# A table of rank shifts in a planned kernel, replaced by another table

## The chip, the cores and the metric

The kernel runs on one core of one Trainium2 chip. The metric is the device time of one execution in microseconds. Before the change the median of 14 runs is 2530.8 us, the lowest 2529.6 and the highest 2535.07.

## The reference, cut to what matters

A block of four residual steps on x of shape (4, 512, 512), each on a layer norm of x: a sparse attention whose mask comes from a small network over all pairs of rows, a feed-forward net, a differential attention, and the same feed-forward net again.

```python
# step 1, sparse attention (D = 512, 32 heads of 2, the 51 best of 512 keys per row)
h    = xn @ W1.T                                                  # 512 x 128 a batch
pair = relu(h[:, :, None, :] - h[:, None, :, :] + b1)             # 512 x 512 x 128
pair = relu(einsum('bijf,gf->bijg', pair, W2) + b2)               # 512 x 512 x 64
sim  = einsum('bijg,og->bijo', pair, W3)[..., 0] + b3[0]
_, top_idx = top_k(sim.at[:, diag, diag].set(0.0), 51)
out  = softmax(q k / sqrt(2) + mask) v @ Wout + bout
# step 2 and step 4, feed-forward (512 -> 2 x 2048 -> 512)
out  = (silu(x Wgate) * (x Wup)) @ Wdown
# step 3, differential attention (16 heads)
out  = softmax(q1 k1 * s - lam * (q2 k2 * s)) v * (1 - li) @ W_proj
```

## The kernel before

**What is tiled how.** For each batch b (0 to 3) and each of its four row tiles, `pair_group` (L751) works on two rows at a time. Two VectorE instructions make the tile `m` (128x512 each), six half-width matmuls (128 rows by 64 columns, fp16 in high and low parts) make `z`, and ScalarE makes `r` from `z`. In five of the sixteen row tiles every fourth group has its `m` made by ScalarE and its `z` by fp32 matmuls. `pair_sums` (L787) then reduces four `r` with four quarter-width matmuls (32 columns, fp32) into `sim`. `topk_tile` (L809) finds the 51 best of a finished `sim` on VectorE in seven rounds, gathers their keys and values with indirect DMAs issued by GpSimd, and does the softmax on VectorE. The feed-forward nets (`ffn`, L931) and the second attention (`attn_b`, L1017) use full-width matmuls, apart from the products with v, which are quarter-width.

A feed-forward net goes over 16 chunks of 128 hidden units. A chunk loads its weights (tile `w`), makes gate and up (`z`), and multiplies the upper half of the rows on with the down weights (accumulators `a`). The other half of its hidden values is stored to DRAM (`hk`) and comes back later (`hc`), with the down weights a second time (`we`), for a second pass (accumulators `b`).

**Names.** Net and attention tiles carry a letter and the batch: f1z is gate and up of the first net of batch 1, e3b the second pass of the second net of batch 3, b2st the scores of the attention of batch 2. `z`, `m`, `r`, `sim` without a letter are the pair work.

**What sets the order.** No engine's order follows the order of the program text. Every operation is first recorded as a task (class `Plan`, L107), with its engine, a cost from a formula (`cost`, L148), the tasks it depends on, and its tiles. `Plan.run` (L261) then plays the whole list as a list scheduler: a free engine takes the ready task of the smallest rank. On TensorE it also models the width of the array in use. To go to another width it waits until all running matmuls have ended and `DRAIN` = 0.1 us more (L327), and tasks of the present width are favoured by `STICK` = 8 (L318). A half-clock state of TensorE, a DMA queue and buffer reuse are modelled too. `Plan.issue` (L363) runs this five times forwards, each time with ranks from a backward run; at the end the ranks of the best plan get a constant added by part of the program, and the list is played once more:

```python
if r > rounds:
    rank = [t + SHIFT.get(part(task[3][0].tensor.name), 0.0) for t, task in zip(best[2], tasks)]
key = {m: min(rank[i] for i in t["tasks"]) for m, t in self.tiles.items()}
tags = {k: (b, sorted(ms, key=key.get) if r else ms) for k, (b, ms) in self.tags.items()}
order, start, length = self.run(rank, after, npre, tags, stick=self.STICK)
if best is None or length < best[0]:
    best = (length, order, rank)
```

So the shifted plan is taken only where the planner holds it shorter. The instructions are then issued in the order of the best plan from one place (L411), so all rows of the profile carry that line; each engine executes its own instructions strictly in that order. A rank is a time in us of the plan, and a shift of +40 lets a part yield to everything whose rank is less than 40 us later.

`part` (L73) maps a tile's name to a key of `SHIFT` (L53). Keys: `f`/`e` with batch and `n` (layer norm), `u`, `v` (chunks 0 to 7 and 8 to 15 of the first pass), `a` (its accumulators), `b` (the second pass); `b` with batch and `n`, `q`, `s`, `t`, `p` (norm, projections, scores, products, output); `p` with batch, row tile and half for the pair groups; `s` for their sums; `k` for the top-k of a row tile; `q`, `a`, `y`, `X` for parts of the preparation and output of step 1; `w` and `c` for scales and constants.

Of the kernel before, what the change touches and what calls it, by code (L numbers as in the profile page):

```python
# [44 lines left out]
def _size(dt):  # L45
# [5 lines left out]


SHIFT = {  # L53
    "X0": -16, "X1": -43, "X2": -35, "X3": -35, "a0": -71, "a1": -41, "a2": -39, "a3": -48, "b0n": 10,
    "b0p": -2, "b0q": 16, "b0s": -14, "b0t": -19, "b1n": -40, "b1p": -36, "b1q": -1, "b1s": -34, "b1t": -37,
    "b2n": 13, "b2q": 16, "b2s": -19, "b2t": -20, "b3n": -17, "b3p": 17, "b3q": -9, "b3s": -25, "b3t": -16,
    "c": -67, "e0a": 36, "e0b": 37, "e0n": 18, "e0u": 22, "e0v": 18, "e1a": -13, "e1b": 31, "e1n": -39,
    "e1u": -27, "e1v": -30, "e2a": 25, "e2b": 439, "e2n": -8, "e2u": -11, "e2v": 15, "e3a": 351, "e3b": 380,
    "e3n": 27, "e3u": 63, "e3v": 260, "f0a": 7, "f0b": 4, "f0n": 21, "f0u": 32, "f1a": -14, "f1n": -36,
    "f1u": -19, "f1v": -33, "f2a": 26, "f2b": 13, "f2n": 27, "f2u": 22, "f2v": 20, "f3a": -18, "f3b": -21,  # L60
    "f3n": -39, "f3u": -48, "f3v": -29, "k00": 13, "k01": 24, "k02": 26, "k03": 12, "k10": 50, "k11": 104,
    "k12": 66, "k13": 25, "k20": 28, "k21": 20, "k22": 19, "k23": 76, "k30": 54, "k31": 59, "k32": 70,
    "k33": 84, "p00u": -9, "p00v": -10, "p01u": 17, "p01v": 16, "p02u": 9, "p02v": 7, "p03u": 6, "p03v": 6,
    "p10u": 6, "p10v": 10, "p11u": 3, "p11v": 6, "p12u": -2, "p12v": -1, "p13u": 10, "p13v": 10, "p20u": 8,
    "p20v": 6, "p21u": -1, "p21v": -3, "p22v": -9, "p23u": -18, "p23v": 17, "p30u": 6, "p30v": 3, "p31u": -11,
    "p31v": -9, "p32u": -6, "p32v": 5, "p33u": 8, "p33v": 49, "q0": -17, "q1": 49, "q2": -87, "q3": -94,
    "s00": -358, "s01": -310, "s02": -192, "s03": -207, "s10": -196, "s11": -177, "s12": -37, "s13": 6,
    "s20": 2, "s21": -7, "s22": -2, "s23": 15, "s30": 1, "s31": -13, "s32": -14, "s33": 5, "w": 84, "y0": -82,
    "y1": 272, "y2": -299, "y3": -48,
}  # L70


# [1229 lines left out]
```

## Time and profile before

| what | value |
|---|---|
| median of 14 runs | 2530.8 us |
| the profiled execution's own time | 2535.03 us |
| its span, first to last instruction | 2533.3 us |
| TensorE busy | 2501.5 us, 15044 matmul records |
| VectorE busy | 2009.6 us |
| ScalarE busy | 1515.8 us |
| GpSimd busy | 966.6 us |
| bytes moved by DMA | 317.79 MB, mean 125 GB/s |

The profiled execution took 4.2 us more than the median, 1.7 us of it outside the span. A matmul that takes 379 ns from start to end does not hold the array that long: in a dense stretch the next starts some 216 ns later, and half-width matmuls run two and quarter-width ones four beside each other. A busy TensorE therefore says only that matmuls were under way.

### The profile page before, as it was taken

How to read it: one execution, taken by the hardware profiler on the slowest of the kernel's cores; microseconds unless marked ns; L12 is line 12 of the kernel's file. 1: busy time of each engine (PE TensorE's matmuls, PEld its weight loads, DVE VectorE, ACT ScalarE, POOL GpSimd, SP SyncE). 2: the span in 40 equal slices, each digit the busy share in tenths (PEclk: the TensorE clock that was granted, in tenths of full speed). 3: DMA queues.
4: the chain of work that ended last, by engine and by line, in shares of the span. 5: the costliest groups of instructions: out<-in, count | busy, mean ns of one | idle time of the engine just before them, and what ended most of it. 6: DMA issues, size and time to landing. Idle time of an engine off the chain costs nothing.

```text
span 2533.3 us, 42662 instructions
## 1 busy us (share of the span) xinstructions
PE 2501.5 (99%) x15044; PEld 1024.6 (40%) x15044; DVE 2009.6 (79%) x5164; ACT 1515.8 (60%) x2831; POOL 966.6 (38%) x847
## 2 busy tenths in 40 slices
PE   8999999999999999999999999999999999999998
PEld 4433333444343334444444333344444443443443
DVE  8889999999899999798686899977856555573531
ACT  6999998656468976443343689643422376586220
POOL 0276767475534155656624234465550000000000
PEclk9999999999999999999999999999999999999999
DMA  5432321157642022336535421034665535423446
GB/s 182 156 106 87 100 63 35 53 163 240 219 136 61 28 65 90 117 116 203 165 94 158 120 53 43 22 115 148 205 206 180 153 120 175 151 95 123 131 144 197
DMA packets 223628, 317.79 MB, mean 125 GB/s; under 512 B 29969, under 2 KB 150865, under 8 KB 222390
## 3 DMA queue, kind: packets, MB, share of 16 engines
q1 hardware_dynamic: 197302, 261.54, 32.4%
q0 software_dynamic: 26112, 53.53, 7.3%
q8 instruction: 118, 1.93, 0.3%
q14 instruction: 96, 0.79, 0.1%
HBM read 263.43 MB, written 51.39 MB: 124 GB/s over the span
## 4 chain that ended last, share of the span: by engine, by line
PE 74%; DVE 19%; DMA 4%; issue 2%; POOL 1%; ACT 1%; SPq 0%; DVEq 0%; POOLq 0%; ACTq 0%
PE z L411 19%; DVE m L411 8%; PE sim L411 6%; PE e0z L411 3%; PE e1z L411 3%; PE e2z L411 3%; PE e3z L411 3%; PE f1z L411 3%; PE f3z L411 3%; PE f2z L411 3%; DVE g L411 3%; PE f0z L411 2%; DVE b1s L411 2%; DVE b0s L411 1%; POOL g L411 1%
## 5 line engine op out<-in xcount | busy, mean ns | idle before, releaser
L411 DVE TENSOR_SCALAR m<-hw 128x512 f32<-128x512 f32 x1888 | 809.8, 483 | 60.3 <-PE z L411 58.5
L411 PE MATMUL z<-m,w2s 128*64 128x512 f16 x5664 | 750.2, 391 | 3.1 <-DVE m L411 1.7
L411 ACT ACTIVATE r<-z,zb 128x512 f32<-128x512 f32 x944 | 613.8, 698 | 222.3 <-PE z L411 160.3
L411 POOL DMA_INDIRECT g<-kv,ix x432 | 494.1, 1144 | 363.8 <-DVE ix L411 212.3
L411 POOL DMA_INDIRECT g<-kv,idx x384 | 461.8, 1203 | 417.7 <-DVE idx L411 197.8
L411 PEld LDWEIGHTS <-w2s 128*64 128x64 f16 x5688 | 315.7, 108 | 491.5 <-issue 227.3
L411 PE MATMUL sim<-r,w 128*32 128x512 f32 x2048 | 274.3, 604 | 0.0
L411 ACT ACTIVATE m<-h 128x512 f32<-128x512 f32 x160 | 107.9, 744 | 5.4 <-PE z L411 5.4
L411 PE MATMUL f3z<-f3xt,f3w 128*128 128x512 f16 x384 | 103.0, 379 | 0.1
L411 PE MATMUL e2z<-e2xt,e2w 128*128 128x512 f16 x384 | 101.5, 379 | 0.0
L411 PE MATMUL f2z<-f2xt,f2w 128*128 128x512 f16 x384 | 98.4, 379 | 0.8 <-DMA f2w<-wf 0.8
L411 DVE TENSOR_TENSOR g<-g,sc 128x832 f32<-128x832 f32 (+3 forms) x128 | 98.5, 783 | 0.3
L411 PE MATMUL z<-m,h 128*64 128x512 f32 x320 | 98.7, 594 | 0.0
L411 PE MATMUL f1z<-f1xt,f1w 128*128 128x512 f16 x384 | 98.3, 379 | 0.0
L411 PE MATMUL f0z<-f0xt,f0w 128*128 128x512 f16 x384 | 90.8, 379 | 0.2 <-ACT f0w L411 0.2
L411 PE MATMUL e0z<-e0xt,e0w 128*128 128x512 f16 x384 | 90.9, 379 | 0.0
L411 PE MATMUL e1z<-e1xt,e1w 128*128 128x512 f16 x384 | 89.5, 379 | 0.0
L411 PEld LDWEIGHTS sim<-r,w 128*32 128x32 f32 x2048 | 41.5, 108 | 115.4 <-issue 96.2
L411 PE MATMUL e3z<-e3xt,e3w 128*128 128x512 f16 x384 | 85.7, 379 | 0.0
L411 DVE MAX8 vm<-sims 128x8 f32<-128x512 f32 x112 | 76.6, 685 | 3.5 <-POOL sims L411 3.0
L411 DVE FIND_INDEX8 ix<-vm,sims 128x8 uint32<-128x512 f32 x112 | 76.4, 682 | 0.0
L411 DVE TENSOR_TENSOR g<-g,q 128x832 f32<-128x832 f32 x64 | 63.9, 999 | 6.7 <-DMA g<-kv,ix 5.6
(643 smaller groups left out, 3779.8 us busy)
## 6 DMA issues: line engine op xcount, KB each, us to landing
f0wr<-wf SPq DMA_DIRECT2D x48, 256.0 KB
wn<-wgu SPq DMA_DIRECT2D x32, 256.0 KB
wf<-f0w SPq DMA_DIRECT2D x16, 512.0 KB
e0w<-wf SPq DMA_DIRECT2D x16, 512.0 KB
f1w<-wf SPq DMA_DIRECT2D x16, 512.0 KB
e1w<-wf SPq DMA_DIRECT2D x16, 512.0 KB
f2w<-wf SPq DMA_DIRECT2D x16, 512.0 KB
f3w<-wf SPq DMA_DIRECT2D x16, 512.0 KB
```

The source lines that it names most:

```text
L411: getattr(eng, op)(*a, **k)
```

## The change

The dictionary `SHIFT` is replaced, and nothing else. The table before has 138 keys, the new one 142; a key that is missing counts as 0. No operation, tile, buffer or dependency is added or removed, and the planner's code and constants stay as they are. What changes are the ranks of the last planning round, and through them the order of instructions on each engine, and which tile takes which buffer when.

New less old value, key by key, has the median +29.5. A constant added to all ranks changes no order, so what counts is the distance from that. Most keys lie within some 20 us of it (the pair groups of batches 1 to 3 at +10 to +41 but for one at -37, the first net of batch 2 at +44 to +52). The ones far from it are these:

| part | old | new |
|---|---|---|
| sums of batch 0, s00 to s03 | -358, -310, -192, -207 | -1313, -1031, -945, -602 |
| top-k k00, k01, k02 | 13, 24, 26 | -325, -46, -58 |
| top-k k21, k22 | 20, 19 | 197, 139 |
| second net of batch 1: e1n, e1u, e1v, e1a, e1b | -39, -27, -30, -13, 31 | 100, 104, 91, 134, 98 |
| second net of batch 2, second pass: e2b | 439 | 230 |
| second net of batch 3: e3n, e3u, e3v, e3a, e3b | 27, 63, 260, 351, 380 | 232, 304, 303, 462, 483 |
| attention output of batch 3: b3p | 17 | 240 |
| keys and values q0, q1, q3 | -17, 49, -94 | -123, 161, 167 |

The diff, cut to some of its lines:

```diff
 SHIFT = {
-    "X0": -16, "X1": -43, "X2": -35, "X3": -35, "a0": -71, "a1": -41, "a2": -39, "a3": -48, "b0n": 10,
...
-    "e1u": -27, "e1v": -30, "e2a": 25, "e2b": 439, "e2n": -8, "e2u": -11, "e2v": 15, "e3a": 351, "e3b": 380,
-    "e3n": 27, "e3u": 63, "e3v": 260, "f0a": 7, "f0b": 4, "f0n": 21, "f0u": 32, "f1a": -14, "f1n": -36,
...
-    "s00": -358, "s01": -310, "s02": -192, "s03": -207, "s10": -196, "s11": -177, "s12": -37, "s13": 6,
...
+    "c": -26, "e0a": 46, "e0b": 46, "e0n": 6, "e0u": 7, "e0v": 54, "e1a": 134, "e1b": 98, "e1n": 100,
+    "e1u": 104, "e1v": 91, "e2a": -1, "e2b": 230, "e2n": 22, "e2u": 31, "e2v": 27, "e3a": 462, "e3b": 483,
+    "e3n": 232, "e3u": 304, "e3v": 303, "f0a": 40, "f0b": 30, "f0n": 34, "f0u": 52, "f0v": 45, "f1a": -9,
...
+    "q1": 161, "q2": -86, "q3": 167, "s00": -1313, "s01": -1031, "s02": -945, "s03": -602, "s10": -129,
...
 }
```

## The prediction

> **What bounds the kernel now.** I read four views. First the page's busy times and its 40 slices: they say which engine has no room.
>
> ```profile
> span 2533.3 us, 42662 instructions
> PE 2501.5 (99%) x15044; PEld 1024.6 (40%) x15044; DVE 2009.6 (79%) x5164; ACT 1515.8 (60%) x2831; POOL 966.6 (38%) x847
> PE   8999999999999999999999999999999999999998
> DVE  8889999999899999798686899977856555573531
> PEclk9999999999999999999999999999999999999999
> ```
>
> TensorE is under way 99% of the span at full clock, VectorE is full in the first half and has room in the second. So the end is set by what TensorE has to do, by how tightly it does it, and in places by VectorE. The second view is TensorE's own waits: who made it idle.
>
> ```profile
> engine line waited for: us in total, times, longest us
> PE f0b L411 <- DMA f0hc<-f0hk: 2.5, 1, 2.5
> PE z L411 <- DVE m L411: 1.7, 5, 0.7
> PE e3b L411 <- DMA e3hc<-e3hk: 1.5, 1, 1.5
> PE e1b L411 <- DMA e1we<-wf: 1.2, 1, 1.2
> PE b1s L411 <- DMA b1qks<-b1qkd: 1.2, 1, 1.2
> ```
>
> The list is short: span less busy time is 31.8 us. From the timeline of TensorE, 8.3 us of that come before 33 us (loading and preparing batch 0), 4.3 after the last matmul. About 19 us of idle time lie in the 2500 us between.
>
> The third view is the timeline of TensorE in a stretch in which only pair work runs.
>
> ```profile
> 1617.43 1.07 PE L411 MATMUL sim<-r,w 128*32 128x512 f32 x8
> 1618.42 3.13 PE L411 MATMUL z<-m,w2s 128*64 128x512 f16 x25
> 1621.48 1.06 PE L411 MATMUL sim<-r,w 128*32 128x512 f32 x8
> 1622.48 2.91 PE L411 MATMUL z<-m,w2s 128*64 128x512 f16 x23
> 1625.32 1.06 PE L411 MATMUL sim<-r,w 128*32 128x512 f32 x8
> ```
>
> This is where the time is that an order can change. Eight fp32 records of quarter width go four beside each other: 2 slots of 512 columns at 1200 a microsecond are 0.85 us, but the next width starts 1618.42 - 1617.43 = 0.99 us later. A stretch of 23 half-width records is 23 x 0.2133 / 2 = 2.45 us and takes 2.84. Each change of the array's width costs something.
>
> I summed this over all 15044 records of the trace. At those rates (512 columns in 0.2133 us for fp16, 0.4267 for fp32, by their share of the array's width) they need 2293 us. The span is 240 us longer. The width changes 936 times; from the last slot's end to the first start of the next width it is 106 ns in the mean, 99 us in all. The rest of the 240 is some 26 us of idle time inside the sequence, 4 after the last matmul, and 111 us inside the stretches: a few ns for each record, and columns that stand empty at a stretch's end.
>
> The fourth view is busy time by stage. Its columns are the window, its length, busy time of TensorE, weight loads, VectorE, ScalarE and GpSimd with instruction counts, clock, DMA share, GB/s.
>
> ```profile
> 33.00:480.00 447.00, 444.99 (x3212) 173.58 (x3211) 428.53 (x1075) 404.41 (x721) 260.11 (x216) 1.00 0.29 93
> 720.00:960.00 240.00, 236.89 (x1628) 87.34 (x1628) 238.77 (x624) 194.78 (x379) 101.61 (x86) 1.00 0.25 75
> 669.00:676.00 7.00, 4.54 (x26) 1.56 (x25) 6.65 (x25) 1.27 (x2) 4.01 (x5) 0.98 1.00 325
> 676.00:679.50 3.50, 3.50 (x10) 1.29 (x11) 2.08 (x8) 1.52 (x2) 2.03 (x3) 0.56 1.06 367
> ```
>
> In the first stage (pair work of batch 0) and under the attentions, VectorE has no idle time worth the name. The last two rows are the one event of their kind: TensorE waits 2.5 us for f0hc with the DMA engines full, and the next 3.5 us run at a granted clock of 0.56.
>
> **The change part by part.** Nothing is added or removed, so the 2293 us of matmul time stay, and so do the 2010 us of VectorE. No instruction and no DMA is new; they are moved past one another. The common drift of about +30 us costs and gives nothing. The rest acts on four terms.
>
> Term 1, width changes. How much can an order alone move? The kernel holds stages of like work, in like company, in different orders. I counted in each the width changes and the time above the 2293 us kind of sum. Second net of batch 0, first and second of batch 1, all under pair work: 34, 30 and 24 changes per 100 us (82, 69 and 49 of them in 242, 229 and 202 us). Attention of batches 0 and 1: 66 and 80 (148 and 159 in 225 and 198 us). If each went at the better twin's density, that is 82 - 58 = 24, 69 - 55 = 14 and 159 - 131 = 28, together 66 fewer; at the worse one, 20, 9 and 31, together 60 more. A change costs 0.106 us of gap at least. From above, the loss per change of whole stages: 15.0 us / 71 changes = 0.21 from 1170 to 1400. Between nets late in the span, 1.8% loss at no change (f2) and 4.0% at 15 per 100 us (f3) make 0.15, which I take. That is -10 us to +9 us. The planner that reads the new table charges 0.1 us for each change, and its operation costs agree with the trace: VectorE's `m` costs 70 + 512/1920 + 60 = 397 ns by its formula and follows its predecessor every 396 ns in the trace; a gather has 1.25 us there and follows its predecessor after 1.255 where nothing holds it up. A table that the planner holds shorter should therefore have fewer changes on the chip too, and an in-order queue doesn't lose that again. I take two thirds of the better end: -7 us.
>
> Term 2, TensorE's 19 us of waits. Bounds: all gone, -19; or as much again, +19. I take 0, because the planner sees such waits in both orders and has left few.
>
> Term 3, the tail. e2b gets 209 less and e3's chunks 43 to 241 more, so e2b goes ahead of e3z instead of standing between e3a and e3b (2476 to 2522 us now). Its 96 matmuls at 0.216 us are 20.7 us that move, not time that is saved. What may vanish are the waits there, 0.9 for e2hc and 1.5 for e3hc: -2.4. What may come is in the slower rival below. I take half of the gain, -1 us.
>
> Term 4, VectorE-bound stages. From 33 to 480 us VectorE is busy 428.5 of 447 us. The top-k of row tile 0 (k00, -338) moves forward within this stage, whose VectorE work is the same; aop, which needs all four top-ks, starts at 441 us now. At best the stage loses its 18.5 us of gaps, at worst as much comes in. That is two-sided, and I take 0. e1 is set back by some 100 us against the pair work beside it (its first pass by 121 to 147, less the 25 of that work). If pair work then ran alone that long, the loss of its stage, 61.7 of 447 us = 13.8%, would stand in place of the 6.3% that I count under e1: +7.5 us. The part of e1 that then runs without pair work goes at f2's 1.8%: -4.5. Together +3 at most; a part with a later rank still fills idle slots, so 0.
>
> The sums of batch 0 (s00 to s03) were 192 to 358 us ahead of everything already; going further ahead alters next to nothing, 0.
>
> Sum: -7 + 0 - 1 + 0 + 0 = -8 us. The profiled execution's 2535.0 would be 2527; on the median, 2530.8 - 8 = 2522.8, and I say 2522.5.
>
> A rule that speaks against this: the Trainium skill, page "TensorE: Matmul & The Clock Gate", Part 1, says that the clock falls to one half after at least one idle window of some 3.4 us, and rises after one busy window. The trace differs: 2.5 us of waiting were enough for 3.4 us at half clock. By the page, new waits under 3.4 us would cost their own length only (2.5 us for one like f0hc); by the row they cost more, which the next part prices.
>
> **The rivals.** (a) Slower: the tail's round trip is exposed. In the chain of waits, e3's second pass waits at the end for its stored halves: a DMA piece of 3.70 and one of 5.35 us. Today e2b's matmuls stand in between and leave 1.5 us visible. With e2b gone, the cover is e3's own earlier chunks. It decides when fewer than 9.05 / 0.216 = 42 matmuls are ready between the last e3z chunk and the load it needs, for instance because the hidden values have five buffers, and loads for later chunks stand behind a store that isn't ready on SP's queue. Then 9.05 us come in, and after such a wait the half clock: the 12 f0b records after the f0hc wait took 4.2 us where 12 x 0.216 = 2.6 are due, so +1.6. Together +10.7. A tail like that is likeliest where term 1 brings nothing either, so I price it alone: 2530.8 + 10.7 = 2541.5. For it: e3b waits here now. Against: 15 earlier chunks have 90 matmuls, 19 us.
>
> (b) The order is no better on the chip: what the plan gained in one place it lost in waits that the plan doesn't price. Three to four small DMA waits of the common size here (0.6 to 1.2 us, as b1s and b0s) weigh up the 8 us with one more of the f0hc kind (2.5 + 1.6). 2531, within 0.2%. For it: the DMA engines are full at some points, where a time by formula must be off. Against: only 19 us of waits in an order from the same planner.
>
> (c) The table doesn't do what it says: if the planner held the shifted list longer than its last unshifted one, the kernel would be issued without shifts. Then term 1 at its worse end: +9, 2540. The code would have to meet a table that fits it badly, so this is small.
>
> (d) Slower by scattered width changes: a plan with fewer waits bought by more changes, again term 1 at its worse end with some waits of term 2: +5 to +15, 2540.
>
> **How the numbers follow.** Forecast, faster by -5 to -20 (the better end of term 1 with part of term 2): 0.47. (b): 0.14. (a): 0.17. (d): 0.18. (c): 0.04. What a measurement of this kernel can tell from no change is about 0.2%, 5 us. Faster 0.47, same 0.14, slower 0.39. The time is that of the likeliest, 2522.5; its own range is 2511 to 2525.7. For 8 in 10: a tenth is left below, -23 us (term 1's 10 and two thirds of term 2's 19), 2508; and a tenth above, (d)'s upper end, 2545.
>
> **What the profile would show.** Term 1: fewer than 936 width changes, near 890, most of it missing under the attentions of batches 0 and 1 and under e0 and f1; the sum of 2293 us unchanged. Term 2: span less busy TensorE time still near 32 us. Term 3: e2b ends before e3z is half done, and e3b alone stands at the end without a wait over 1.5 us. Term 4: VectorE's work from 33 us to the first aop the same, that stage ending within 10 us of now. A wait of e3b for e3hc of 5 us or more speaks for (a); new rows of 2 us with stretches of half clock for (b); more than 960 changes for (c) or (d). The forecast is wrong if the changes don't fall, or if they fall and the idle time grows by as much.

## The result, and the profile after

The changed kernel is slower: 2555.6 us median (2552.77 to 2557.21) against 2531.4 for the kernel before, measured in alternation with it. The ratio is 1.0092 (95% interval 1.0082 to 1.0102). The forecast was 2522.5, faster, with a range of 2508 to 2545; sign and range are both wrong.

What the two pages share, seen after:

```profile
span 2556.4 us, 42718 instructions
...
PE 2504.0 (98%) x15044; PEld 1028.0 (40%) x15044; DVE 2019.1 (79%) x5164; ACT 1517.4 (59%) x2831; POOL 970.3 (38%) x847
...
PE   8999999999999999999999999999999999999999
...
DVE  8799999999999999886778999996666556475332
...
PEclk9999999999999999999999999999999999999999
```

The slices show nothing: 23.1 us in 2556 are spread too thin for tenths. The sum does. Span less busy time of TensorE was 31.8 us and is 52.4, which makes 20.6 us of new idle time. TensorE's time at half clock rose from 6.25 to 18.2 us. The last of it (2.84 us before, 1.11 after) lies behind the last matmul and costs nothing. In the rest TensorE did 1.7 us of matmul work before and 6.2 after, which took twice as long there, so 4.5 us more are lost. There are 856 width changes instead of 936. Without the waits that end at a few of them, which are idle time and counted already, their gaps fell from 93.6 to 85.0 us: -8.5. The 2293 us of matmul time are the same. That makes 16.6 of the 23.1 us; the other 6.5 lie inside the stretches of one width and are not split up here. TensorE's own waits name the new idle time:

```profile
engine line waited for: us in total, times, longest us
PE z L411 <- DVE m L411: 6.7, 11, 2.5
PE e1b L411 <- DMA e1we<-wf: 5.6, 7, 1.7
PE zp L411 <- DVE hw L411: 5.3, 2, 4.9
PE e1z L411 <- DMA e1w<-wf: 3.5, 2, 2.2
PE b1s L411 <- DMA b1qks<-b1qkd: 2.8, 1, 2.8
PE f0b L411 <- DMA f0we<-wf: 2.0, 2, 1.1
```

Before, `z<-m` stood at 1.7 us, e1we at 1.2, b1qks at 1.2, and zp and e1w were not among the first. No single wait explains it: VectorE is late with `m`, and loads are late in several places.

Where in time? I compared the two runs at equal matmul work done (the running sum of the 2293 us). After is 5.5 us behind when 25 us of work are done; 6.8 at 125, 15.9 at 225 and 25.8 at 325, which is 411 us into the run. It gets some back, holds 16 to 20 us until 1475 us of work, and goes to 23 at 1675 and about 25 at the end. So there are three places.

**The start.** These are TensorE's timeline rows (start, duration, engine, line, operation, count, idle before and releaser) of after, with two windows of busy time by engine:

```profile
32.34 0.42 PE L411 MATMUL zp<-hw,w2s 128*64 128x256 f16 x2 [4.93 <-DVE hw L411]
...
1768.28 2.65 PE L411 MATMUL e1z<-e1xt,e1w 128*128 128x512 f16 x7 [2.24 <-DMA e1w<-wf]
```

```profile
28.00:38.20 10.20, 5.64 (x28) 2.99 (x30) 8.31 (x24) 9.43 (x23) 0.00 (x0) 0.50 0.83 300
1700.00:1822.00 122.00, 118.52 (x587) 52.11 (x582) 86.52 (x210) 41.20 (x75) 66.94 (x66) 0.99 0.52 158
1822.00:1900.00 78.00, 72.17 (x337) 32.73 (x336) 50.68 (x103) 15.26 (x28) 44.64 (x43) 1.00 0.74 230
```

Around a wait of 4.93 us TensorE runs 10.2 us at a granted clock of 0.50 (first window): the clock falls 0.6 us after the wait has begun and rises some 6 us after it has ended. The plan holds this delay too and is still 4.6 us shorter than the old one.

**150 to 410 us.** The top-k of batch 0 gathers its rows with GpSimd's indirect DMAs, and VectorE's products wait for them. VectorE's and then GpSimd's timeline rows of one such case, after:

```profile
243.22 0.74 DVE L411 SCALAR_TENSOR_TENSOR f0w<-f0wr,sc,f0w 128x512 f16<-128x512 f32 x1
246.25 1.03 DVE L411 TENSOR_TENSOR g<-g,q 128x832 f32<-128x832 f32 x1 [2.29 <-DMA g<-kv,ix]
```

```profile
229.86 1.09 POOL L411 DMA_INDIRECT g<-kv,idx  x1 [1.42 <-DVE idx L411]
231.26 4.97 POOL L411 DMA_INDIRECT g<-kv,idx  x1 [0.30 <-issue]
```

One gather took 4.97 us instead of the 1.0 of its neighbours, the queue behind it is late, and VectorE stands 2.29 us. VectorE is the full engine of this stage and its queue is in order: `m` is late, and then `z`. The group row of these products tells the sum over the whole run (busy, mean ns, idle before and its causes), before and then after:

```profile
L411 DVE TENSOR_TENSOR g<-g,q 128x832 f32<-128x832 f32 x64 | 63.9, 999 | 6.7 <-DMA g<-kv,ix 5.6 <-issue 1.0
```

```profile
L411 DVE TENSOR_TENSOR g<-g,q 128x832 f32<-128x832 f32 x64 | 63.9, 999 | 24.6 <-DMA g<-kv,ix 11.2 <-issue 11.0 <-DMA g<-kv,idx 2.3
```

The same rows up to 410 us alone, before and then after:

```profile
L411 DVE TENSOR_TENSOR g<-g,q 128x832 f32<-128x832 f32 (+1 forms) x13 | 13.0, 997 | 0.3 <-DMA g<-kv,ix 0.3
```

```profile
L411 DVE TENSOR_TENSOR g<-g,q 128x832 f32<-128x832 f32 (+1 forms) x12 | 12.0, 1000 | 8.3 <-DMA g<-kv,ix 5.1 <-issue 3.2
```

So 8.3 of the 24.6 us belong to this stage. "issue" stands for a wait whose end the profile puts down to nothing. Here it is a wait for gathers too: 10.7 of the 11.0 us lie under a wait of VectorE's queue for the semaphores of the gathers.

Long gathers are no more frequent than before (over 2 us: 29 of 816 before, 32 after). Nor are they random: in after_half_w (experiment 4), which issues the same order, 31 of these 32 gathers are over 2 us again, 28 of the 32 within 0.3 us of their time here. What differs in the plan is the room: 19 of the 64 products stood within 0.5 us of the planned landing of their last gather before, 39 after.

**1700 to 1900 us.** In the two last windows above TensorE is busy 118.52 and 72.17 us. The same windows before:

```profile
1700.00:1822.00 122.00, 120.72 (x683) 50.07 (x680) 93.86 (x234) 50.52 (x84) 65.33 (x61) 1.00 0.52 161
1822.00:1900.00 78.00, 77.24 (x362) 35.23 (x361) 49.48 (x104) 15.06 (x32) 45.37 (x44) 1.00 0.69 216
```

The shares of the DMA engines (last column but one) are alike or a little higher after. e1 now begins at 1708 us instead of 1641 and overlaps f2, which begins at 1827 in both, until 1891 instead of 1843; the waits for e1w and e1we lie here.

### The profile page after: what moved, and what is told of

Its sections match the earlier page's. It is cut to its first block, busy times and chain, and to the rows that moved or that the text cites. A ratio compares the mean times of both kernels' runs of the same rounds, so it can differ in the third digit from the quotient of the medians.

```text
span 2556.4 us, 42718 instructions
## 1 busy us (share of the span) xinstructions
PE 2504.0 (98%) x15044; PEld 1028.0 (40%) x15044; DVE 2019.1 (79%) x5164; ACT 1517.4 (59%) x2831; POOL 970.3 (38%) x847
## 3 DMA queue, kind: packets, MB, share of 16 engines
q1 hardware_dynamic: 197302, 261.54, 32.2%
## 4 chain that ended last, share of the span: by engine, by line
PE 70%; DVE 16%; DMA 5%; POOL 4%; issue 4%; ACT 1%; SPq 0%; DVEq 0%; POOLq 0%; ACTq 0%
PE z L411 17%; DVE m L411 7%; PE sim L411 6%; POOL g L411 4%; PE e0z L411 3%; PE e2z L411 3%; PE e3z L411 3%; PE f1z L411 3%; PE f3z L411 3%; PE f0z L411 3%; PE e1z L411 3%; PE f2z L411 2%; DVE g L411 2%; DVE b0s L411 1%; DVE b1s L411 1%
## 5 line engine op out<-in xcount | busy, mean ns | idle before, releaser
L411 ACT ACTIVATE r<-z,zb 128x512 f32<-128x512 f32 x944 | 606.7, 695 | 192.7 <-PE z L411 145.1
L411 POOL DMA_INDIRECT g<-kv,idx x384 | 467.1, 1216 | 378.3 <-DVE idx L411 212.1
L411 PE MATMUL sim<-r,w 128*32 128x512 f32 x2048 | 279.6, 604 | 0.0
L411 PEld LDWEIGHTS sim<-r,w 128*32 128x32 f32 x2048 | 44.1, 108 | 118.3 <-issue 102.5
L411 DVE TENSOR_TENSOR g<-g,q 128x832 f32<-128x832 f32 x64 | 63.9, 999 | 24.6 <-DMA g<-kv,ix 11.2
```

Source lines behind the costliest of these rows:

```text
L411: getattr(eng, op)(*a, **k)
```

## Two measures that the experiments use

The planner calls the old order 2501.2 us long and the new one 2496.6. It is 4.6 us better by the planner's account, as intended, and 24.2 worse on the chip. I call chip median less planned length the **excess**: 30.2 us before, 59.0 after. To see where it grows I set each ScalarE and VectorE instruction's start in the trace against its planned start (median within 8 us of the plan time named):

| plan time, us | 200 | 300 | 400 | 720 | 1200 | 1600 | 1900 | 2300 |
|---|---|---|---|---|---|---|---|---|
| before | 2.2 | 3.1 | 3.7 | 11.7 | 18.6 | 25.4 | 27.8 | 32.2 |
| after | 4.9 | 12.2 | 15.0 | 17.5 | 23.5 | 33.7 | 47.6 | 56.6 |

The theory takes the new table to come from a search on planned length alone, which used up whatever room the old order had between one engine's planned end and the next engine's planned start. The planner has one fixed time for a gather and a handover and one formula for a load. On the chip they differ from case to case, and every lateness then shows. Room costs planned length, so that a search for length removes it.

## The experiments

**1. No table, and both tables with a little noise.** `SHIFT` is emptied; or every value of the old or the new table gets a normal deviate of 0.03 us, which reorders near-ties and breaks what is finely fitted.

```diff
-SHIFT = {
...
-}
+SHIFT = {}
```

> SHIFT is empty, so the kernel is issued in the planner's last unshifted order, whose planned length is 2550.1 us (the table before: 2501.2, the new one: 2496.6). Call slip the measured median less the planned length: 30 us before, 59 after. Theory (the new table used up the margin in front of waits whose real length the planner doesn't know; how much an order slips depends on its margin): an order that no search has squeezed slips less than the new one, 30 to 48 us, so 2580 to 2598. Rival (every order of this planner slips by some 59 us, and the one before was a lucky one): 2609, at least 2602.

> The table before with every shift moved at random by 0.03 us in the mean; planned length 2502.0. Theory (margin belongs to the region of the table): slip stays near 30, 2530 to 2540. Rival (the table before is one lucky order): slip near 59, 2555 to 2565.

> The new table with every shift moved at random by 0.03 us in the mean; planned length 2502.1, the same as the table before with such noise. Theory: slip near 59, 2555 to 2565, so some 25 us longer than the other at equal planned length. Rival (the new table is one unlucky order): slip near 30 to 40, 2532 to 2542.

Measured: without a table 2599.2 us (ratio 1.0247, 1.0227 to 1.0267) on a plan of 2550.1, an excess of 49.1, between the two cases and 1 us above what was expected, with before 3.1 us up beside it. The old table with noise 2535.7 (1.0006, 0.9996 to 1.0016), the new one with noise 2570.2 (1.0138, 1.0119 to 1.0156), 5 us above its band, on planned lengths of 2502.0 and 2502.1. At one planned length the chip puts 34.5 us between them. So the loss doesn't hang on one finely fitted accident of the new order: it belongs to the region of tables around the new one. Products waited 1.0 us with the old noisy table, 25.6 with the new one. Without a table they waited 3.2 us, although 33 of the 64 stood within 0.5 us of the planned landing: the count of such products alone doesn't tell the wait.

**2. Are the long gathers caused by VectorE?** The Trainium skill, page "SBUF — State Buffer", section "SBUF: two separate sides", says that VectorE in certain modes and GpSimd shut each other out of a shared port, for the length of an instruction. If gathers of 2 to 6 us came from rows of `m` without a break, a tiny other VectorE instruction after every fourth `m` should shorten them.

```diff
                 getattr(eng, op)(*a, **k)
+                if key == "DVE":
+                    run = run + 1 if re.match(r"m\d_", a[0].tensor.name) else 0
+                    if run == 4:
+                        eng.tensor_tensor(self.gap, self.gap, self.gap, ALU.mult)
+                        run = 0
```

> The changed kernel in its own order, but after every four m instructions that stand one behind another on VectorE a 128x1 multiply of a scratch tile. Theory (GpSimd's gathers that last over 2 us, 32 of 816, are held while VectorE runs m without a break, and the products that stand just behind them on VectorE then wait, 25 us in all): gathers over 2 us fall under 15, the idle time before the products under 15 us, and the time to 2540 to 2550, less what the added instructions cost. Rival (the long gathers have another cause): their number stays, time 2556 to 2566.

Measured: gathers over 2 us 29 against 32, over 3 us 6 against 11, idle time before the products 21.1 against 24.6, 2572.3 us (1.0158, 1.0127 to 1.019). What the theory expected was missed on every count, and the 300 added multiplies of 0.15 us cost time themselves.

Gather by gather the run says more. In 11 of the 32 long gathers of after, `m` makes up three quarters or more of VectorE's work while the gather lasts. Of these 11, 10 take under 2 us here, and their mean falls from 3.3 to 1.5 us; in after_half_w, the same order without the breaks, 10 of the 11 are over 2 us and the mean is 3.3. Of the other 21, which lie under less `m` and more of VectorE's other work, all 21 stay over 2 us in both. So rows of `m` without a break do lengthen the gathers beside them, in agreement with the page's rule; that a port is the way isn't seen in the trace. What lengthens the other 21 stays open.

**3. Room at the gathers, at the loads, at both.** The new table stays. In the last planning round alone the planner takes a gather to need 7 us instead of 4, or a load on SyncE's queue 1 us more, or both.

```diff
-                    end = max(queue, t + 1.6 + 1.5 * self.xfer[i])
+                    end = max(queue, t + 1.6 + self.more + 1.5 * self.xfer[i])
...
+                self.more = 1.0
+                after = [[(j, 7.0 if lag == 4.0 else lag) for j, lag in a] for a in after]
```

> The new table, but in the last planning round the planner takes a gather to land 7 us after its issue in place of 4, so that the order leaves room in front of the products. Its order has a length of 2509.3 us by the old constants (2496.6 as changed). Theory (the missing margin is in front of gathers and of loads): the idle time before the products falls from 25 us under 8, and slip (median less the length by the old constants) from 59 to 40 to 48, so 2549 to 2557: no longer than the changed kernel although the plan is 12.7 us longer. Rival (margin doesn't matter, the new order is bad by other things such as column filling): slip stays at 59 or more, at least 2568.

> The new table, but in the last round the planner takes every DMA issued by SP to land 1 us later. Length by the old constants 2519.2. Theory: the waits of TensorE for weights under e1 and f2 (16 us in the changed kernel by the slip from 1620 to 1900 us) mostly go, those before the products stay; slip 42 to 50, 2561 to 2569. Rival (loads have nothing to do with it): slip 59, 2578.

> Both together. Length by the old constants 2516.7. Theory: slip 25 to 34 as with the table before, 2542 to 2551, less than the changed kernel though its plan is 20 us longer. Rival: slip 59, 2576.

Measured, with planned lengths by the old constants, before at 2535.8 beside them, and the excess by plan time below:

| kernel | planned | median | ratio, 95% | idle before products |
|---|---|---|---|---|
| after_gather7 | 2509.3 | 2567.9 | 1.0126, 1.0102 to 1.0149 | 5.8 |
| after_load1 | 2519.2 | 2560.2 | 1.0095, 1.0076 to 1.0114 | 9.1 |
| after_both | 2516.7 | 2561.0 | 1.0103, 1.0087 to 1.0120 | 1.9 |

| plan time, us | 200 | 300 | 400 | 720 | 1200 | 1600 | 1900 | 2300 |
|---|---|---|---|---|---|---|---|---|
| after_gather7 | 3.3 | 3.6 | 3.8 | 8.8 | 14.0 | 28.7 | 42.1 | 52.4 |
| after_load1 | 1.4 | 6.4 | 7.0 | 11.9 | 18.9 | 26.0 | 29.6 | 34.7 |
| after_both | 1.8 | 3.9 | 4.3 | 9.2 | 14.2 | 20.5 | 28.0 | 32.7 |

Held room takes lateness away where it is held. With room at the gathers the product row of after_gather7 has this left:

```profile
L414 DVE TENSOR_TENSOR g<-g,q 128x832 f32<-128x832 f32 x64 | 63.8, 997 | 5.8 <-issue 5.4 <-DMA g<-kv,ix 0.4
```

and the excess at 400 us falls from 15.0 to 3.8, that of before. But past 1200 us it grows as in after, and the same kernel's waits of TensorE name the loads there:

```profile
PE b1s L414 <- DMA b1qks<-b1qkd: 4.0, 2, 2.2
...
PE e1z L414 <- DMA e1w<-wf: 2.5, 2, 2.1
PE e1b L414 <- DMA e1we<-wf: 2.2, 2, 1.7
PE f2z L414 <- DMA f2w<-wf: 2.1, 1, 2.1
```

With room at the loads the late growth goes, and 34.7 us at 2300 is close to the 32.2 of before. But room at the loads alone also brings the excess at 400 us down to 7.0 and the products' waits to 9.1 us: a change of the whole order acts in other places too. For the time, after_load1 came out as expected (41.0 us of excess, 1 below its band), and the other two missed. after_gather7 has an excess of 58.6 us, that of the rival, since what it gained early it lost late; after_both has 44.3, where 25 to 34 were expected. Where the excess fell from 59.0, to 41.0 and 44.3, the plans became 22.6 and 20.1 us longer: with this table, held room costs as much as it saves.

**4. The stage at e1 and f2 by itself.** After's order, but for these two nets only the high halves of the gate and up weights are loaded, and the matmuls of the low halves read the high ones in their place.

```diff
+                        if name in HALF:
+                            plan.alt[len(plan.tasks)] = (z, w[:, 0, g, k, :], xt[:, j, k, :])
```

> The changed kernel in its own order; the gate and up weights of the nets e1 and f2 are loaded in their high half alone, and the matmuls with the low half use the high one (so the low parts of two nets are left out of the result): 256 KB a chunk in place of 512. Theory (from 1700 to 2000 us TensorE waits for weights that the DMA engines deliver later than planned): those waits fall by most of their size, time lower by 7 to 12 us, 2544 to 2549. Rival (they come from the order of SP's queue, or from VectorE): lower by at most 3 us, 2553 or more.

The two windows of this run (compare with those of after and before above):

```profile
1700.00:1822.00 122.00, 121.57 (x642) 53.41 (x637) 93.70 (x234) 48.00 (x85) 69.47 (x68) 1.00 0.43 122
1822.00:1900.00 78.00, 74.55 (x349) 34.10 (x348) 51.92 (x105) 17.14 (x32) 46.20 (x44) 1.00 0.73 215
```

TensorE gets 121.57 and 74.55 us instead of 118.52 and 72.17, and the excess gained between plan times 1700 and 1900 falls from 13.9 to 5.7 us. Over the same matmul work (from 1490 to 1765 us of its running sum) TensorE loses 12.3 us before, 19.9 after and 10.7 here. The median, 2554.1 (1.0069, 1.0052 to 1.0086), is 1.5 us below after's and by itself in the rival's band; with before 4.4 us up beside it the gain is about 6, where 7 to 12 were expected. So late weights are shown as the cause in this stage, and it holds about a quarter of the loss.

**5. Extra delay on GpSimd in both orders.** Four small memsets on GpSimd ahead of every fourth gather, in before and in after.

```diff
+                if op == "indirect_dma_start":
+                    seen += 1
+                    if seen % 4 == 0:
+                        for _ in range(4):
+                            eng.memset(self.gap, 1.0)
```

> The kernel before, its order untouched; GpSimd sets a 128x64 scratch tile four times (about 0.5 us) ahead of every fourth gather. Both orders get the same disturbance. Theory (the order before has more room in front of the products): longer by 10 to 30 us. Rival (both have the same room): as much as the changed kernel under the same disturbance, within 5 us.

> The changed kernel, its order untouched, with the same four settings ahead of every fourth gather. Theory: longer than the changed kernel by 25 to 60 us, and by at least 10 us more than the kernel before grows. Rival (same room in both): grows by the same, within 5 us.

Measured: 2545.0 (1.0030, 1.0019 to 1.0042) and 2569.1 (1.0120, 1.0100 to 1.0140), with before at 2536.3 beside them: +8.7 for the old order, and +8.6 for the new one (2569.1 - 2555.6, less the 4.9 us that before was up). The idle time before products grew by 7.3 and 9.0 us. A miss for the theory: delays put in by hand cost both orders alike. So the old order isn't shown to have more room against any lateness, only against the one that the chip has as it is. Nor is the disturbance a pure delay: gathers over 2 us went from 29 to 15 and from 32 to 23.

**6. Searching again, from the old table.** searched_alone is a search on planned length alone, in 12,410 trials. searched_margin is one in 12,147 with gathers at 5 us and loads 0.25 us longer in the last round.

> A table searched from the one before in 12,147 trials (one shift or one group moved at a time, shorter plans kept), while the planner's last round takes gathers to land 1 us later (5 in place of 4) and SP's transfers 0.25 us later. Length of its order by the old constants 2485.1. Theory (a plan searched with margin keeps its gain on the chip): slip 22 to 32 us as with the table before, so 16 us shorter than it less some: 2508 to 2518 where the kernel before takes 2531, a ratio of 0.991 to 0.995. Rival (any further search on this planner is lost on the chip): slip 45 or more, 2531 or longer.

> The same search from the same table, 12,410 trials, on the planned length alone with the planner's own constants; planned length 2492.5, 8.7 us shorter than the table before. Theory: the gain is bought with margin, slip 36 to 50, 2529 to 2542, a ratio of 0.999 to 1.005. Rival (a search on the length alone does no harm, the new table was unlucky): slip 25 to 32, 2518 to 2525, a ratio under 0.998.

These and the later runs met chips on which before takes 2561 to 2563 us. What differs is seen in the waits of ScalarE and VectorE, though not for before itself, of which no profile was kept there. These are rows of the changed kernel's profile from experiment 7, ScalarE first, where "issue" is a wait for nothing that the profile shows and "remote" one for an unknown queue:

```profile
ACT r L411 <- issue: 16.2, 11, 5.6
...
ACT e0t L411 <- issue: 13.8, 5, 4.0
...
ACT f2hb L411 <- issue: 13.8, 1, 13.8
```

```profile
DVE g L411 <- issue: 12.0, 6, 5.0
...
DVE f2t L411 <- issue: 11.1, 5, 4.4
...
DVE e1t L411 <- remote: 8.3, 2, 5.0
```

All rows of the two kinds together are 120.2 us on ScalarE and 64.3 on VectorE; in the first profile of after they are 9.3 and 11.3, in that of before 0.3 and 1.0. Of the 9.3 and 11.3 us, 7.4 and 10.7 lie under a wait of the engine's queue for a semaphore; of the 120.2 and 64.3 only 14.9 and 10.7. So on these chips the engines stand for some other reason, and the excess is compared with that of before on the same chip. Measured: searched_margin 2573.4 (1.0050, 1.0032 to 1.0068) on a plan of 2485.1, searched_alone 2593.3 (1.0130, 1.0109 to 1.0150) on one of 2492.5. The search on length alone lost too, by more than the change did and by more than expected. The one with a little room came out 16.1 us shorter in the plan than before, and still lost 11 us to it: a miss, on the side of its rival.

**7. Room at every handover.** Four kernels on one chip. searched_slack continues searched_margin's search with gathers at 5 us, loads 0.25 us and handovers between engines 0.03 us longer; searched_slack_more has 0.5 and 0.05. In searched_replayed the planner is untouched and only the table differs; each of 10,599 trials was scored by how long its fixed order takes when gathers need 5 us, loads 0.3 us more and handovers 0.05 us more. after_again is the changed kernel.

```diff
+                self.more = 0.25
+                after = [[(j, 5.0 if lag == 4.0 else lag + (0.03 if 0 < lag < 1 else 0)) for j, lag in a] for a in after]
```

> The planner's last round holds a gather at 5 us, a load of SyncE's queue 0.25 us longer and every handover from one engine to another 0.03 us longer, and the shifts are searched again under that (13,953 trials more). By the constants of before the planned length is 2491.0 us, against 2501.2 before and 2496.6 after. Theory (the search has used up the room at every planned handover, and the loss is that room): with room held at gathers, loads and handovers the excess of the chip's time over the plan returns to about that of before, 30 to 38 us, so the time is 0.993 to 1.000 of before's on the same chip. Rival (a searched table loses to before whatever room the plan holds, from something that the plan doesn't model): an excess of 45 us or more, 1.003 to 1.010 of before's.

> As searched_slack, with more room in the last round: gather 5 us, loads 0.5 us longer, handovers 0.05 us longer. Planned length by the constants of before 2501.7 us, that of before within 0.5 us. Theory: an excess at or below that of before, 25 to 35 us, so 0.996 to 1.003 of before's time. Rival: 45 us or more, 1.005 to 1.012.

> The table alone is changed, the planner not at all: the shifts are searched from the table of before in 10,599 trials, each plan scored not by its own length but by the length of its fixed order when gathers take 5 us, loads 0.3 us longer and handovers 0.05 us longer. Planned length 2494.7 us, 1.9 us less than after and 6.5 less than before. Theory: the excess is that of before or less, 28 to 36 us, so 0.993 to 1.000 of before's time and below that of after. Rival: as after, 1.005 to 1.010.

> The changed kernel itself, on the chip of the three others, as their control. Both theories: 1.007 to 1.014 of before's time on that chip.

| kernel | planned | median | ratio, 95% | excess above that of before |
|---|---|---|---|---|
| searched_slack | 2491.0 | 2595.2 | 1.0122, 1.0094 to 1.0150 | 44.1 |
| searched_slack_more | 2501.7 | 2569.5 | 1.0031, 1.0015 to 1.0046 | 7.7 |
| searched_replayed | 2494.7 | 2566.2 | 1.0016, 0.9996 to 1.0036 | 11.4 |
| after_again | 2496.6 | 2592.6 | 1.0112, 1.0090 to 1.0134 | 35.9 |

(Before: 2561.3, an excess of 60.1.) searched_slack_more loses 0.3%, and searched_replayed can't be told from before, where after loses 1.1%. searched_replayed and searched_alone start from one table, get about as many trials and issue through the same planner; the score differs, and the ratios are 1.0016 and 1.0130, on two chips of the disturbed kind. It is one search for each score, so chance isn't excluded. after_again is where it was expected; searched_slack_more is just above its 0.996 to 1.003, searched_replayed above its 0.993 to 1.000 but below the rival's 1.005, and the excesses of all four are far above their bands, as is that of before. searched_slack is a plain miss: it has room at each kind of handover, and it lost the most of the four. The score of searched_replayed, worked out for other tables with the planner alone and without a run, is right for some and not for all: 2527.9 us for before and 2550.7 for after, 22.8 apart where the chip has 24.2, but 2495.3 for searched_slack, which should have made it the best.

**8. The same two again.** To see whether the standing engines were the reason, searched_slack and searched_replayed ran once more.

> The same kernel as searched_replayed, a second time. On the chip of that run, VectorE and ScalarE stood some 64 and 120 us with nothing to wait for that the profile shows (about 1 us together in the profile of before), and before itself took 2561 us. On a chip where before takes 2531 to 2537 us: theory (the loss is room that the search used up; this table was chosen for room) an excess over the plan of 28 to 38 us, 0.995 to 1.001 of before; rival (a searched table loses to before on any chip) 1.005 or more. On a chip where before takes 2550 us or more: again 1.000 to 1.004, which tells nothing new.

> The same kernel as searched_slack, a second time: it lost 1.2% there, against the theory, on a chip with standing engines. On a chip where before takes 2531 to 2537 us: theory (what beat it there was the standing of engines, which room at gathers, loads and handovers doesn't cover) 0.993 to 1.003 of before; rival (the room that the planner holds in its last round doesn't help the chip at all) 1.008 or more. On a chip where before takes 2550 us or more: again 1.009 to 1.015, which tells nothing new.

Measured: 2569.2 (1.0026, 1.0003 to 1.0048) and 2597.4 (1.0134, 1.0091 to 1.0177), with before at 2562.6: again such a chip, so nothing new, as the expectations say. Of 47 stands over 1 us of ScalarE and VectorE in slack_again, 28 are at the same instruction, within 0.3 us of the same length, in searched_slack. Most are not random, but I haven't found what they wait for.

## Why the prediction was wrong

**Term 1, width changes (-7).** Right in size. There are 856, where near 890 was forecast, but not all in the places named: from its first to its last matmul the attention of batch 0 has 21 more, that of batch 1 42 fewer, and e1, which now runs with little pair work, 42 fewer. The price of 0.15 us was too high. Even the 106 ns in the mean hold some waits that end at a change; the 923 changes without a wait take 98.9 ns before, the 847 after 98.6. So 80 fewer are worth 8 us. The 0.15 came from comparing whole stages, where the changes stand beside other losses.

**Term 2, waits of TensorE (0).** This is the step that failed. It says "I take 0, because the planner sees such waits in both orders and has left few". They came to +20.6 us of idle time and +4.5 through the half clock, above the +19 that I had set as its upper end. Term 1 leans on the same belief: "A table that the planner holds shorter should therefore have fewer changes on the chip too, and an in-order queue doesn't lose that again". The first half of that sentence held, the second didn't. The planner sees a wait only where its fixed times produce one. Where an order has just enough room for these times, the planner shows no wait and the chip shows many small ones. I had tested the planner's costs on `m` and on the start-to-start time of gathers, and both agree; it is how long single gathers and loads take that varies: the planner gives each gather the same time, and 32 of 816 take over 2 us instead of 1.0, mostly the same ones in a second run of the order. I didn't look at how near the old order was to its limits.

**Term 3, the tail (-1).** The way that was forecast, and more of it. After is 26.2 us behind at 2225 us of work and 23.0 at 2290. e2b's last matmuls now come at 2435 us, no wait of e3b or e2b for a load is among those of TensorE, and the loss in e3's own stage fell from 4.9 to 1.5 us.

**Term 4, VectorE-bound stages (0, bounds of 18.5).** After lost 20 us here between 25 and 325 us of work, a little beyond the bound. 11.3 of them are excess (15.0 against 3.7 at plan time 400), behind products that wait for gathers; the other 9 are in the plan itself, and 9 come back by 625. The first aop stands at 480.7 us instead of 441.7, where a stage end within 10 us of the old was forecast. e1 was to cost +3 at most. Its stage and f2's lost 15.8 and 11.9 us to other things than matmul slots, against 12.7 and 2.7 before; they overlap, and over the same matmul work it is +8 (19.9 against 12.3), which late weights explain (experiment 4).

**The rivals.** (a), the tail's round trip, didn't occur. (b) had the right mechanism, waits that the plan doesn't price, at a third of the size: "three to four small DMA waits". I let it cancel term 1 and never asked what it would be if the search had looked for such places. (c) is out, since the shifted plan is the shorter one (2496.6 against 2550.1) and without a table the kernel takes 2599 us. (d) is out, since width changes fell. The text's own warning came true: fewer changes, and more idle time than they saved.

**The clock.** Here 2.24 us of waiting for e1w were followed by 3.4 us at a granted clock of 0.52, and 2.52 us of waiting for `m` at 273 us by 3.4 us at half clock, as the 2.5 us wait was before. A wait of 2.79 us for b1qks was not: from 1443 to 1450 us the granted clock is 1.00. Around the wait of 4.93 us the half clock held 10.2 us, some 6 of them with matmuls running. The rule of the Trainium skill, page "TensorE: Matmul & The Clock Gate", Part 1, asks for one idle window of some 3.4 us; three waits here were shorter and cost the clock all the same, so the length of a wait alone doesn't decide.

**What stays open.** That the loss is lateness at gathers and loads is shown in its two places (experiments 3 and 4), but no run took the whole loss back: 9 of the 29 us by which the excess grew come after 1900 us of the plan and weren't looked into. Which keys of the table do it wasn't tried. That the choice of the score makes the difference is supported by searched_replayed against searched_alone, one search each on disturbed chips, and not shown. What kind of room is needed stays open: searched_slack has room by the planner's account and loses 1.2%. Whether a searched table with room beats before on an undisturbed chip wasn't measured; no version here beat it.

## What to carry to other kernels

A list scheduler's length is a forecast with an error, and a search on it alone can end at orders for which that error is large: the new table bought 4.6 planned microseconds and cost 24 measured ones, and searched_alone, a search on length alone, bought 8.7 and cost 31. The error needn't be chance; here the same gathers were late again when the order was issued again. Score candidates under late transfers and late handovers too, look at how many planned starts lie within a fraction of a microsecond of their releaser, and run the best few on the chip before keeping one. When a change of order is forecast from a planner, the term to size is the waits that the planner can't see.

## What the runs showed of the hardware

Indirect gathers mostly keep GpSimd 1.0 us each, but 15 to 44 of 816 take over 2 us in every profile, the longest of a profile 3.6 to 6.4 us. Which ones depends mostly on the order: of after's 32, 31 came back in after_half_w and 25 in after_again. VectorE's rows of `m` are one cause: with a break after every fourth, 10 of the 11 long gathers under `m` fell below 2 us, and none of the other 21. A change of the array's width takes 99 ns where no wait ends at it (923 changes before, 847 after). Times differ by 1%: before took 2531 to 2536 us beside experiments 1 to 5 and 2561 to 2563 beside 6 to 8, on other chips and later, which can't be told apart here. There ScalarE and VectorE stand for nothing that the profile names, up to 5.6 us at a time (`r` in after_again).
